# SP's order of reads and loads, the place of the block transpose, and row maxima over two banks in a perceiver layer's kernel

## The chip, the cores and the metric

The kernel runs on one core of a Trainium2 chip. The metric is the device time of one execution in microseconds. Time before: 3738.01 us, the median of 3 runs (3735.43 to 3746.63). One further execution was profiled; it took 3731.84 us, and every duration below comes from it.

The core's engines each work through a list of their own: TensorE (PE, with its weight loads PEld), VectorE (DVE), ScalarE (ACT), GpSimd (POOL) and SyncE (SP). SP computes nothing: it issues the transfers (DMAs) one after the other, and an instruction of SP that has to wait holds all that stand behind it.

## The reference

One layer on x (16 sequences of 128 rows, 512 wide), with a context of 2048 rows for each sequence, all in float32. It has three parts, each added to x after a layernorm:

```
q = ln(x) @ wq.T + bq;  k = ctx @ wk.T + bk;  v = ctx @ wv.T + bv      # 16 heads of 32
x = x + softmax(q k^T / sqrt(32)) v @ wo.T + bo                        # attention
x = x + mamba_block(ln(x))     # in_proj, causal conv, selective scan over 16 states, out_proj, then an MLP
x = x + expert_mix(ln(x))      # softmax gate, top 2, one shared and one expert matrix
```

The change lies in the attention: the scores, the softmax, and the product of the probabilities with v.

## The kernel before, in words

The work is one stream of steps (the loop at L1329). Step u handles one sequence, one quarter of its context (512 rows) and one group of four heads: 16 x 4 x 4 = 256 attention steps (NU), "live" in the code. Behind them, 54 steps later, runs the selective scan of the sequences whose attention is done; the projections in and out, the normalizations and, after step 256, the MLP and the experts are fitted into the steps by tables that map a step to functions (`loads`, `late`, `behind`, `inner` and others, filled by `put`, L1205 on). The schedule is manual: each engine gets its instructions in the order in which the program writes them, and waits are added where data or buffers need them. A tile with n buffers waits for the last reader of the tile that had its buffer before.

A step does this, in the program's order:

- SP: `load_bc` of the scan's first factor, at u % 4 of 1 or 2 the next context tiles (`load_ctx`), the table `loads` (x, weights and others), then the second `load_bc` (L1337 to L1352).
- `scores` (L302): TensorE writes four heads' scores into four PSUM banks, `banks[0..3]`, 128 rows x 512 each.
- `weighted` (L379): TensorE multiplies the probabilities of step u - 1 with v. For heads 0 to 2 they were turned on TensorE (`turn`, L354: four transposes into the head's bank, a copy to pT on ScalarE). The fourth head takes another way: VectorE transposes it in blocks of 32 (`blocks`, L334), SP writes the result to a DRAM buffer trd, and four reads bring it back in the wanted order as pd (`gathered`, L344). This head is used one step later still: step u uses the pd of u - 2.
- `gathered(u - 1)` (L1362): SP's four reads. They wait for trd's write, and for TensorE's reading of the one pd buffer in this step's `weighted`.
- `maxima` (L312): VectorE, one reduction for each bank, negated. `x_products` (L278): TensorE, two products for the k or v of the next context quarter, into the PSUM tiles pa and pc. k and v are made by a scheme of seven products and sums of quarters; each takes two steps (phase 0 and 1).
- `exps` (L319): ScalarE, one exp for each bank with the negated maximum as bias; the row sums come along.
- `inputs` on GpSimd, then the first half of the scan on VectorE (`scan(g, r, 0)`, L727: a scan, a product with bc, a memset).
- `blocks(u)` on VectorE (L1395), with SP's write to trd; `hold` copies pa on ScalarE; `decays(g, r, 1)` are two exps for the scan's second half; then `x_sums` on VectorE (L1403) adds pc and the held copy. pc can be written again after that.
- `turn` for heads 0 to 2, the second half of the scan, the `late` work (projections and the like, which use banks[3] first, then the others, pc or avp as their place), `behind` (`dt_first`, L660: a product, read by ScalarE and VectorE, in pc while k or v are made), and at the end `y_products` and `y_sums`.

The weights share one ring of six tiles of 256 KB (tag "ws", WS = 6): wq and wo (`load_w`), win for the scan's input projection (`load_win`, two a step), wout for its output (`load_wout`, six at a time). Their users are in the `late` table of the following step.

Of the kernel before, what the change touches and what calls it, by code (L numbers as in the profile page):

```python
# [15 lines left out]
P = 128  # L16
# [20 lines left out]
def perceiver_layer(ctx: ExitStack, tc: tile.TileContext, a: dict, out: bass.AP):  # L37
# [75 lines left out]
    with ExitStack() as es:  # L113
# [12 lines left out]

        banks = [psum.tile([P, 512], FP, tag=f"s{j}", name=f"bank{j}") for j in range(4)]
        avp = psum.tile([P, 4, P], FP, tag="av", name="avp")  # L130
        hst = psum.tile([P, NH // 2, GT], FP, tag="h0", name="hst")
        pa = psum.tile([P, 2, 256], FP, tag="pa", name="pa")
# [33 lines left out]
        def load_w(i, b):  # L166

            for c in range(KC):
                t = ssm.tile([P, KC, P], FP, tag="ws", name=f"wqo{i}_{b}_{c}", bufs=WS)
                if i == 0:  # L170
                    nc.sync.dma_start(t, a["wqkvo"][i][:, :, c * P : (c + 1) * P])
                else:
                    nc.sync.dma_start(t.rearrange("p a b -> p (a b)"), a["wqkvo"][i][:, c, :])
                wts_in[i, b, c] = t
# [113 lines left out]
        def x_sums(of, g, ph, pa, pc):  # L288
            sums[of](g, ph, ph, pc, held[of])
# [21 lines left out]

        def maxima(u):  # L312
            b, sb, hg = split(u)
            for j in range(4):
                nc.vector.tensor_reduce(  # L315
                    stats[b][0][j][:, sb, hg : hg + 1], banks[j], AX.X, ALU.max, negate=True
                )

        def exps(u):  # L319
            b, sb, hg = split(u)  # L320
            nm, sm = stats[b]
            pr = pool.tile([P, 4, 512], FP, tag="pr", name=f"pr{u}", bufs=1)
            for j in range(4):
                h = hg * 4 + j
                nc.scalar.activation(  # L325
                    pr[:, j, :],
                    banks[j],
                    AF.Exp,
                    bias=nm[j][:, sb, hg : hg + 1],
                    accum_out=sm[:, sb, h : h + 1],  # L330
                )
            prs[u] = pr

        def blocks(u):  # L334

            t = pool.tile([P, 4, ND, 4, 32], FP, tag="tr", name=f"tr{u}", bufs=1)
            for h in range(ND):
                nc.vector.transpose(  # L338
                    t[:, :, h].rearrange("p c i q -> p i c q"),
                    prs[u][:, NP + h, :].rearrange("p (i c k) -> p i c k", i=4, c=4),  # L340
                )
            nc.sync.dma_start(trd[u % 2], t.rearrange("p c h i q -> p (c h i q)"))

        def gathered(u):  # L344
# [70 lines left out]
        def normal(b):  # L415

            x = xts[b]
            root_third(rstd[:, b : b + 1], *xts.pop((b, "r")))
            xn = keep.tile([P, D], FP, tag="aT", name="xn", bufs=1)
            nc.vector.tensor_scalar(  # L420
                xn, x, mv[:, b, 0:1], rstd[:, b : b + 1], ALU.subtract, ALU.mult
            )
            if b:
                nc.gpsimd.tensor_tensor(x, x, bo, ALU.add)
            xts[b, "n"] = xn
            nm = [keep.tile([P, SB, 4], FP, tag=f"nm{j}", name=f"nm{b}_{j}") for j in range(4)]
            sm = keep.tile([P, SB, H], FP, tag="sm", name=f"sm{b}")
            stats[b] = nm, sm

# [31 lines left out]
        def joined(b):  # L461

            parts, sm = stats[b]
            nm = keep.tile([P, SB, H], FP, tag="nm", name=f"nm{b}")
            for j in range(4):
                nc.vector.tensor_copy(
                    nm.rearrange("p s (k j) -> p s k j", j=4)[:, :, :, j], parts[j]
                )
            stats[b] = nm, sm

# [74 lines left out]
        def load_win(g, i):  # L545

            t = ssm.tile([P, KC, P], FP, tag="ws", name=f"win{g}_{i}", bufs=WS)
            nc.sync.dma_start(t, a["win"][i // 4][:, :, (i % 4) * P : (i % 4 + 1) * P])
            wts_in[g, i] = t
# [650 lines left out]


        early = {}
        late, after, inner, middle, loads, head, behind, between = ({} for _ in range(8))

        def put(where, u, f):  # L1205
            where.setdefault(u, []).append(f)

        for b in range(B):
            s = 16 * b
            if b:  # L1210
                put(loads, s - 8, lambda b=b: load_x(b))
                put(loads, s - 5, lambda b=b: load_w(0, b))
                put(inner, s - 8, lambda b=b: moments_of(b))
                put(middle, s - 7, lambda b=b: root_of(b))
                put(inner, s - 7, lambda b=b: normal(b))
                put(late, s - 4, lambda ps, b=b: queries(b, ps))
            e = s + 16
            put(loads, e + 5, lambda b=b: load_w(3, b))
            put(inner, e - 1, lambda b=b: joined(b))
            put(inner, e, lambda b=b: joined_first(b))  # L1220
            put(middle, e + 1, lambda b=b: shares(b))
            put(inner, e + 1, lambda b=b: joined_second(b))
            put(head, e + 2, lambda b=b: joined_third(b))
            for sb in range(SB):
                put(inner, e + 2 + (sb > 0), lambda b=b, sb=sb: spread_out(b, sb))
                put(late, e + 3 + (sb > 0), lambda ps, b=b, sb=sb: scaled(b, sb, ps))
            put(late, e + 6, lambda ps, b=b: attended(b, ps))
            put(middle, e + 7, lambda b=b: root_of(b))
            put(inner, e + 7, lambda b=b: normed(b))
            put(late, e + 8, lambda ps, b=b: z_turned(b, ps))  # L1230
        for g in range(NG):
            p = 32 * (g + 1)
            for ec in range(EC):
                put(loads, p + 8 + ec, lambda g=g, ec=ec: load_win(g, ec))
                put(loads, p + 8 + ec, lambda g=g, ec=ec: load_win(g, EC + ec))
                put(late, p + 9 + ec, lambda ps, g=g, ec=ec: x_part(g, ec, ps))
                put(late, p + 9 + ec, lambda ps, g=g, ec=ec: z_part(g, ec, ps))
                put(after, p + 10 + ec, lambda g=g, ec=ec: silu_first(g, ec, xas))
                put(after, p + Z_GATES[ec], lambda g=g, ec=ec: silu_first(g, ec, zss))
            put(late, p + 18 + (g == NG - 1), lambda ps, g=g: x_proj(g, ps))  # L1240
            s = p + LAG
            for ec in range(EC):
                put(loads, s - 4 + 4 * ec, lambda ec=ec: load_dtproj(ec))
                put(behind, s - 3 + 4 * ec, lambda ps, g=g, ec=ec: dt_first(g, ec, ps))
                put(middle, s - 2 + 4 * ec, lambda g=g, ec=ec: dt_second(g, ec))
                put(between, s - 1 + 4 * ec, lambda g=g, ec=ec: dt_third(g, ec))
            for i in range(GB):
                for ec in range(WS):
                    put(loads, s + 32 + 2 * i, lambda g=g, i=i, ec=ec: load_wout(g, i, ec))
                put(loads, s + 31 + 2 * i, lambda b=g * GB + i: reload_x(b))  # L1250
                put(late, s + 33 + 2 * i, lambda ps, g=g, i=i: projected(g, i, ps))

# [76 lines left out]
        for u in range(last):  # L1329
# [4 lines left out]
            made, phase = divmod(u + 3, 4)  # L1334
            makes = 0 < made < B * SB
            of, phase = ("k", "v")[phase // 2], phase % 2
            load_bc(u + 2 - 32 - LAG, 0)  # L1337
            if u % 4 == 1 and made + 1 < B * SB:
                load_ctx(made + 1, ("c00", "c10", "c11"))
            if u % 4 == 2 and made + 1 < B * SB:  # L1340
                load_ctx(made + 1, ("c01",))
            for f in loads.get(u, ()):
                f()
            if scans and u <= NU:
                decays(g, r, 0)
            if u > NU:
# [2 lines left out]
                    fed += 1  # L1349
                if scans:  # L1350
                    decays(g, r, 0)
            load_bc(u + 1 - 32 - LAG, DS)  # L1352
            if u == NU + 1:
                load_rows()
            if live:
# [1 line left out]
            if 1 <= u <= NU:  # L1357
                weighted(u - 1, range(4))
                if u > 1:
                    weighted_last(u - 2)  # L1360
                weighted_out(u - 1)
                gathered(u - 1)  # L1362
            for f in early.get(u, ()):
                f()
            if u == NU:
# [25 lines left out]
            silu_third()  # L1391
            if scans:
                scan(g, r, 0)
            if live:
                blocks(u)  # L1395
            if live and u % 4 == 2:
                values_kept(u // 4)
            if makes:
# [2 lines left out]
                decays(g, r, 1)  # L1401
            if makes:
                x_sums(of, made, phase, pa, pc)  # L1403

# [8 lines left out]

            ahead = live and u % 16 in (3, 10) and len(after_turns) == 1
            if ahead:
                after_turns[0](banks[3])
                after_turns, places = (), ()
            if live:  # L1420
                for j in range(NP):
# [10 lines left out]
                    f(ps)  # L1432
                    give_back(ps)
            for f in behind.get(u, ()):
                ps = flat(pc) if makes else banks[2] if live else bank()
                f(ps)
                if not live:
                    give_back(ps)
# [84 lines left out]
```

## Time and profile before

| | |
|---|---|
| profiled execution | 3731.84 us |
| its span, first to last instruction | 3730.1 us |
| median of the runs | 3738.01 us |
| mean granted TensorE clock | 0.992 |
| step 0 starts / step 255 starts | 42.15 / 3041.25 us |
| one reduction of 128 x 512 (L315), 1024 of them | 681 ns |
| one exp of 128 x 512 (L325), 1024 of them | 686 ns |
| the block transpose of 128 x 512 (L338), 256 of them | 711 ns |
| first sum of a k part, 128 x 256 (L264), 256 of them | 461 ns |
| the same of v, 128 x 512 (L274), 126 of them | 663 ns |
| bc load, 512 KB, issue to landing (median) | 4.9 us |
| pd read, 64 KB, issue to landing (median) | 2.6 us |
| SP waits at the pd reads for TensorE | 555.9 us, 209 times |

A line of a view names engine, source line, operation, out<-in, and the number of instructions (x8). In the timeline the first two numbers are the start and the length in us of a run of such instructions, and in brackets stands the engine's idle time before it and what ended it. In the list of waits the numbers are the sum in us, how often, and the longest. In the windows view follow, after the stretch and its length, the busy times of PE, PEld, DVE, ACT and POOL, then the granted clock of TensorE (1.00 is full), the busy share of the DMA engines, and GB/s. "SPq" is SP's queue. Times written as "scores + 5.6" are counted from the start of a step's first scores matmul.

### The profile page before, as it was taken

The page shows a single profiled execution, that of the slowest core. Times are in us where ns is not written, and L with a number is a line of the kernel's source. Part 1 is how long each engine was busy: PE and PEld are TensorE (multiplying, and loading weights), DVE is VectorE, ACT ScalarE, POOL GpSimd, SP SyncE. Part 2 cuts the span into 40 slices and gives each one's busy share as a digit, 9 for nine tenths or more (in the row PEclk, how much of TensorE's full clock was granted, in tenths as well). Part 3 has the DMA queues.
Part 4 walks back from the last instruction along what each step waited for, and adds up shares of the span by engine and source line. Part 5 has one row for each costly group of instructions (what it writes and reads, how often), then busy time and mean ns, then how long its engine had stood idle before and what let it go on. Part 6 is the DMA issues. An engine that isn't in the chain of part 4 may idle for free.

```text
span 3730.1 us, 71240 instructions
## 1 busy us (share of the span) xinstructions
PE 3643.5 (98%) x25096; PEld 2762.6 (74%) x25096; DVE 2712.5 (73%) x4902; ACT 2423.5 (65%) x5928; POOL 2135.2 (57%) x2097
## 2 busy tenths in 40 slices
PE   9999999999999999999999999999999989999999
PEld 7878787777777877778777867787777766655655
DVE  4444546887778787878687878877887777778843
ACT  4555556776677776777686767776777675545432
POOL 2111114774767576766676667666675667667820
PEclk9999999999999999999999999999999999999999
DMA  4323334565566556565756565656565668577752
GB/s 126 94 91 97 114 97 145 188 210 160 190 209 201 182 188 204 184 195 166 223 181 198 166 226 177 193 173 218 187 199 177 205 208 320 196 272 240 249 191 81
DMA packets 527556, 682.76 MB, mean 183 GB/s; under 512 B 44848, under 2 KB 378960, under 8 KB 526944
## 3 DMA queue, kind: packets, MB, share of 16 engines
q1 hardware_dynamic: 526752, 677.57, 56.5%
q8 instruction: 200, 3.28, 0.4%
q14 instruction: 156, 1.28, 0.1%
q0 software_dynamic: 448, 0.63, 0.1%
HBM read 594.40 MB, written 83.62 MB: 182 GB/s over the span
## 4 chain that ended last, share of the span: by engine, by line
PE 91%; DMA 3%; DVE 2%; ACT 1%; SPq 1%; issue 1%; POOL 0%; DVEq 0%; ACTq 0%; POOLq 0%
PE pa L244 24%; PE pc L244 17%; PE bank L358 8%; PE avp L386 7%; PE bank L307 7%; PE bank L575 5%; PE bank L986 4%; PE bank L955 3%; PE bank L760 2%; PE bank L1087 2%; DMA pd<-trd 2%; PE bank L516 2%; PE bank L443 1%; PE avp L986 1%; PE pa L955 1%
## 5 line engine op out<-in xcount | busy, mean ns | idle before, releaser
L315 DVE TENSOR_REDUCE nm<-bank 128x1 f32<-128x512 f32 x1024 | 634.9, 681 | 263.8 <-PE bank L307 263.1
L747 POOL TENSOR_TENSOR ysum<-ysum,w 128x512 f32<-128x512 f32 x384 | 499.9, 1302 | 453.3 <-DVE hst L710 262.3
L325 ACT ACTIVATE pr<-bank,nm 128x512 f32<-128x512 f32 x1024 | 689.1, 686 | 65.9 <-DVE nm L315 61.1
L696 POOL TENSOR_TENSOR w<-dx,bc 128x512 f32<-128x512 f32 x512 | 654.7, 1300 | 8.9
L731 DVE TENSOR_TENSOR_SCAN hst<-hst,w 128x512 f32<-128x512 f32 x459 | 561.0, 1222 | 43.7 <-ACT hst L717 39.2
L717 ACT ACTIVATE hst<-dt,alog 128x254 f32<-128x254 f32 x918 | 440.1, 479 | 79.2 <-DVE hst L710 63.9
L360 ACT COPY pT<-bank 128x512 f32<-128x512 f32 x768 | 396.6, 587 | 51.3 <-PE bank L358 51.0
L358 PE MATMUL bank<-ident,pr 128*128 128x128 f32 x3072 | 378.2, 273 | 0.8 <-ACT pr L325 0.7
L358 PEld LDWEIGHTS bank<-ident,pr 128*128 128x128 f32 x3072 | 350.5, 141 | 26.3 <-ACT pr L325 3.0
L386 PEld LDWEIGHTS avp<-pT,v 128*32 128x32 f32 x6144 | 206.5, 110 | 193.7 <-issue 193.0
L734 DVE TENSOR_TENSOR w<-hst,bc 128x512 f32<-128x512 f32 x459 | 317.2, 691 | 20.9 <-DMA bc<-bcd 5.3
L236 POOL TENSOR_TENSOR t<-c,c 128x512 f32<-128x512 f32 x128 | 164.3, 1284 | 239.9 <-PE pc L244 235.1
L307 PE MATMUL bank<-kt,qT 32*128 32x512 f32 x2048 | 295.7, 640 | 0.7 <-ACT pT L360 0.7
L386 PE MATMUL avp<-pT,v 128*32 128x128 f32 x6144 | 280.8, 277 | 0.0
L338 DVE STREAM_TRANSPOSE tr<-pr 128x512 f32<-128x512 f32 x256 | 182.1, 711 | 102.2 <-ACT pr L325 101.2
L244 PE MATMUL pa<-vs,t 128*128 128x256 f32 x1008 | 252.5, 395 | 0.0
L244 PE MATMUL pa<-t,ks 128*128 128x256 f32 x1024 | 248.6, 386 | 0.0
L386 PE MATMUL avp<-pd,v 128*32 128x128 f32 x1536 | 206.4, 278 | 38.1 <-DMA pd<-trd 38.1
L244 PEld LDWEIGHTS pa<-vs,t 128*128 128x128 f32 x1008 | 190.7, 195 | 37.1 <-issue 11.9
L244 PEld LDWEIGHTS pa<-t,ks 128*128 128x128 f32 x1024 | 185.9, 190 | 36.0 <-issue 14.2
L325 ACT ACTIVATION_READ_ACCUMULATOR pr<-bank,nm 128x1 f32 x1024 | 208.5, 204 | 0.0
L623 POOL TENSOR_TENSOR xa<-xa,sg 128x256 f32<-128x256 f32 x64 | 46.7, 729 | 263.7 <-ACT sg L622 263.7
(321 smaller groups left out, 7524.3 us busy)
## 6 DMA issues: line engine op xcount, KB each, us to landing
bc<-bcd SPq DMA_DIRECT2D x512, 512.0 KB, 4.9
c<-in_ctxT_dram SPq DMA_DIRECT2D x256, 256.0 KB, 4.8
trd<-tr SPq DMA_DIRECT2D x256, 256.0 KB, 2.1
pd<-trd SPq DMA_DIRECT2D x1024, 64.0 KB, 2.6
wf<-in_w_dram SPq DMA_DIRECT2D x124, 512.0 KB, 6.7
wqo<-in_wqkvo_dram SPq DMA_DIRECT2D x128, 256.0 KB, 5.3
win<-in_win_dram SPq DMA_DIRECT2D x128, 256.0 KB, 5.0
wout<-in_wout_dram SPq DMA_DIRECT2D x128, 256.0 KB, 4.1
```

Of the source, the lines that this page charges most:

```text
L244: nc.tensor.matmul(ps[:, r, :], l[:, kc, r * P : (r + 1) * P], m[:, kc, :], start=(i in (1, 2, 5) and r == 0 and kc == 0), stop=(r == 1 an ...
L307: nc.tensor.matmul(banks[j], qts[b][rows, hg, :], kts[u // 4, hg][rows, :], start=True, stop=True)
L315: nc.vector.tensor_reduce(stats[b][0][j][:, sb, hg : hg + 1], banks[j], AX.X, ALU.max, negate=True)
L325: nc.scalar.activation(pr[:, j, :], banks[j], AF.Exp, bias=nm[j][:, sb, hg : hg + 1], accum_out=sm[:, sb, h : h + 1],)
L358: nc.tensor.transpose(ps[:, i, :], prs[u][:, j, i * P : (i + 1) * P], ident)
L360: nc.scalar.copy(pT, ps)
L386: nc.tensor.matmul(avp[j * HD : (j + 1) * HD, v % 4, :], values(v, i, j), pts[v, j][:, i, :] if j < NP else pds[v][:, :, j - NP, i, :], st ...
L696: nc.gpsimd.tensor_tensor(w, dx.unsqueeze(1).to_broadcast([P, NH // 2, GT]), bcs[g * 32 + r, 0][:, i * NH // 2 : (i + 1) * NH // 2, :], AL ...
L717: nc.scalar.activation(bt(h[:, k, :])[:, :, 1:], bt(dt)[:, :, 1:], AF.Exp, scale=aneg[:, ec, n : n + 1],)
L731: nc.vector.tensor_tensor_scan(flat, flat, w.rearrange("p n t -> p (n t)"), 0.0, ALU.mult, ALU.add)
L734: nc.vector.tensor_tensor(w, h, bcs[g * 32 + r, DS][:, i * NH // 2 : (i + 1) * NH // 2, :], ALU.mult)
L747: nc.gpsimd.tensor_tensor(s, s, w, ALU.add)
```

## The change

- **SP's order.** In steps 1 to 256 the loads of a step no longer come first. They become `step_loads`, called after `gathered(u - 1)`: the table `loads`, both `load_bc`, then `load_ctx`. The weights of the ring move to a table of their own, `weights`, which runs at the end of the engines' middle part, behind trd's write. In the steps after 256 the weights go with `step_loads` at the start of the step, and both `load_bc` stand behind them, ahead of what `feed` loads.
- **VectorE's order.** `blocks(u)` comes after `x_sums` (and after `decays` and `values_kept`), no longer ahead of them. The transpose itself is one call for all its heads; with one such head it is the same instruction as before.
- **Maxima.** The four banks become two PSUM tiles of two banks each; `banks[j]` is a slice of one. `maxima` makes two reductions of 128 x 2 x 512 in place of four of 128 x 512. The statistics tiles and their joining change with it (two copies in place of four).
- **Places.** `dt_first` uses banks[3], where a step has no late work, and otherwise its place of before. The line with `after_turns[0](free[0])` names the same bank as before (NP is 3).

```diff
-        banks = [psum.tile([P, 512], FP, tag=f"s{j}", name=f"bank{j}") for j in range(4)]
+        pairs = [psum.tile([P, 2, 512], FP, tag=f"s{m}", name=f"bank{m}") for m in range(2)]
+        banks = [pairs[j // 2][:, j % 2, :] for j in range(4)]
...
-            for j in range(4):
+            for m in range(2):
                 nc.vector.tensor_reduce(
-                    stats[b][0][j][:, sb, hg : hg + 1], banks[j], AX.X, ALU.max, negate=True
+                    stats[b][0][m][:, sb, hg, :], pairs[m], AX.X, ALU.max, negate=True
                 )
...
-                    bias=nm[j][:, sb, hg : hg + 1],
+                    bias=nm[j // 2][:, sb, hg, j % 2 : j % 2 + 1],
...
-            for h in range(ND):
-                nc.vector.transpose(
-                    t[:, :, h].rearrange("p c i q -> p i c q"),
-                    prs[u][:, NP + h, :].rearrange("p (i c k) -> p i c k", i=4, c=4),
-                )
+            nc.vector.transpose(
+                t.rearrange("p c h i q -> p (h i) c q"),
+                prs[u][:, NP:, :].rearrange("p h (i c k) -> p (h i) c k", i=4, c=4),
+            )
...
-                put(loads, s - 5, lambda b=b: load_w(0, b))
+                put(weights, s - 5, lambda b=b: load_w(0, b))
...
-            put(loads, e + 5, lambda b=b: load_w(3, b))
+            put(weights, e + 5, lambda b=b: load_w(3, b))
...
-                put(loads, p + 8 + ec, lambda g=g, ec=ec: load_win(g, ec))
-                put(loads, p + 8 + ec, lambda g=g, ec=ec: load_win(g, EC + ec))
+                put(weights, p + 8 + ec, lambda g=g, ec=ec: load_win(g, ec))
+                put(weights, p + 8 + ec, lambda g=g, ec=ec: load_win(g, EC + ec))
...
-                    put(loads, s + 32 + 2 * i, lambda g=g, i=i, ec=ec: load_wout(g, i, ec))
+                    put(weights, s + 32 + 2 * i, lambda g=g, i=i, ec=ec: load_wout(g, i, ec))
...
-            load_bc(u + 2 - 32 - LAG, 0)
-            if u % 4 == 1 and made + 1 < B * SB:
-                load_ctx(made + 1, ("c00", "c10", "c11"))
-            if u % 4 == 2 and made + 1 < B * SB:
-                load_ctx(made + 1, ("c01",))
-            for f in loads.get(u, ()):
-                f()
+
+            def step_loads():
+                for f in loads.get(u, ()):
+                    f()
+                for f in weights.get(u, ()) if u > NU else ():
+                    f()
+                load_bc(u + 2 - 32 - LAG, 0)
+                load_bc(u + 1 - 32 - LAG, DS)
+                if u % 4 == 1 and made + 1 < B * SB:
+                    load_ctx(made + 1, ("c00", "c10", "c11"))
+                if u % 4 == 2 and made + 1 < B * SB:
+                    load_ctx(made + 1, ("c01",))
+
+            if not 1 <= u <= NU:
+                step_loads()
...
-            load_bc(u + 1 - 32 - LAG, DS)
...
                 gathered(u - 1)
+                step_loads()
...
-            if live:
-                blocks(u)
...
             if makes:
                 x_sums(of, made, phase, pa, pc)
+            if live:
+                blocks(u)
+            for f in weights.get(u, ()) if u <= NU else ():
+                f()
...
-                after_turns[0](banks[3])
+                after_turns[0](free[0])
...
-                ps = flat(pc) if makes else banks[2] if live else bank()
+                n = len(late.get(u, ()))
+                if live and n < len(free):
+                    ps = free[n]
+                else:
+                    ps = flat(pc) if makes else banks[2] if live else bank()
```

More of the change, by code (lines that the diff above doesn't have):

```diff
@@ L425, in normal @@
             xts[b, "n"] = xn
-            nm = [keep.tile([P, SB, 4], FP, tag=f"nm{j}", name=f"nm{b}_{j}") for j in range(4)]
+            nm = [
+                keep.tile([P, SB, 4, 2], FP, tag=f"nm{m}", name=f"nm{b}_{m}") for m in range(2)
+            ]
             sm = keep.tile([P, SB, H], FP, tag="sm", name=f"sm{b}")
@@ L464, in joined @@
             nm = keep.tile([P, SB, H], FP, tag="nm", name=f"nm{b}")
-            for j in range(4):
+            for m in range(2):
                 nc.vector.tensor_copy(
-                    nm.rearrange("p s (k j) -> p s k j", j=4)[:, :, :, j], parts[j]
+                    nm.rearrange("p s (k m j) -> p s k m j", m=2, j=2)[:, :, :, m, :], parts[m]
                 )
@@ L1202, in perceiver_layer @@
         early = {}
-        late, after, inner, middle, loads, head, behind, between = ({} for _ in range(8))
+        late, after, inner, middle, loads, head, behind, between, weights = ({} for _ in range(9))
         def put(where, u, f):
```

## The prediction

> **What bounds it now.** First the page: engines, then the chain that ended last.
>
> ```profile
> PE 3643.5 (98%) x25096; PEld 2762.6 (74%) x25096; DVE 2712.5 (73%) x4902; ACT 2423.5 (65%) x5928; POOL 2135.2 (57%) x2097
> ...
> PE 91%; DMA 3%; DVE 2%; ACT 1%; SPq 1%; issue 1%; POOL 0%; DVEq 0%; ACTq 0%; POOLq 0%
> ```
>
> TensorE carries the end, and its idle time is only 3730.1 - 3643.5 = 86.6 us. So a gain must come out of that time, or out of matmuls that run slow. Next, the waits of TensorE:
>
> ```profile
> PE avp L386 <- DMA pd<-trd: 40.1, 16, 3.8
> PE pc L244 <- DVE kt L264: 7.4, 8, 1.2
> ```
>
> Half of the idle time is one wait: the fourth head's probabilities (pd) come late from DRAM. The timeline shows where. TensorE in step 108 (a step runs from one group of scores, L307, to the next):
>
> ```profile
> 1248.18 1.14 PE L307 MATMUL bank<-kt,qT 32*128 32x512 f32 x8
> 1249.26 0.42 PE L386 MATMUL avp<-pT,v 128*32 128x128 f32 x6
> 1252.17 0.27 PE L386 MATMUL avp<-pd,v 128*32 128x128 f32 x1 [2.49 <-DMA pd<-trd]
> ...
> 1253.74 3.01 PE L244 MATMUL pa<-vs,t 128*128 128x256 f32 x8
> ```
>
> and SP's queue before it:
>
> ```profile
> 1228.42 3.85 SPq L171 DMA_DIRECT2D wqo<-in_wqkvo_dram  x4
> 1244.40 2.27 SPq L548 DMA_DIRECT2D win<-in_win_dram  x2
> 1246.76 0.57 SPq L645 DMA_DIRECT2D bc<-bcd  x1
> 1247.38 1.85 SPq L348 DMA_DIRECT2D pd<-trd  x4
> ```
>
> From 1232.27 to 1244.40 SP waits to load win: its ring of six tiles is full until the in_proj of 1242.48 has read one. The four reads of pd stand behind it, although their data lay ready. In step 119 six wout loads (L553) do the same. The gaps at pd lie in steps 12 and 23 of every 32 (u mod 32), twelve in all, 36.7 us.
>
> A stall costs more than itself: the 8 products after this one took 3.01 us, elsewhere 1.89 to 1.99. The windows view of 10 us around stalls has the granted clock after the engines:
>
> ```profile
> 1250.00:1260.00 10.00, 7.83 (x58) 6.72 (x59) 5.90 (x10) 6.03 (x18) 2.58 (x3) 0.83 0.31 102
> 862.00:872.00 10.00, 6.99 (x43) 5.70 (x43) 4.37 (x7) 4.98 (x14) 1.88 (x3) 0.66 0.33 110
> 1006.00:1016.00 10.00, 7.67 (x59) 6.08 (x60) 6.35 (x10) 5.82 (x17) 2.13 (x3) 1.00 0.69 239
> ```
>
> 0.83 over 10 us is 1.7 us lost, 0.66 is 3.4, 1.00 nothing. Nine of the twelve windows read 0.83, two 0.66, one 1.00: 9 x 1.7 + 2 x 3.4 = 22.1 us.
>
> The Trainium skill ("TensorE: Matmul & The Clock Gate", section "What's actually happening") says the clock falls to half after an idle window of about 3.4 us. Here nine of the ten stalls shorter than that were followed by a slow window, so the rows overrule it. By the rule only the stalls of 3.45 and 3.77 us would pay, 3.4 us in all, and the first term below would be about 20 us smaller.
>
> **The change, part by part.**
>
> *1. SP's order: gathers first, weights last.* In step u (1 to 256) SP now has the four reads of pd (u-1), then loads, bc and ctx, then trd's write, then weights. The waits for the ring (win, wout, wqo) no longer stand ahead of the reads within a step. They could only delay the next step's reads, and those wait for its weighted anyway (scores + 2.2 us). Worst cases by step time: in 11 the second win waits for in_proj until +10.5, SP is free at 11.2, the next reads are due at 12.66 + 2.2; in 22 wout waits for the out projection until +10.4, next reads at 13.9 + 2.2. So the stalls go whole. Their size by step length: step 108 took 22.03; step 92 with the same queries but no in_proj took 14.07, and an in_proj pair adds 3.45 (step 109's 12.22 less step 117's 8.77), so 17.52. The six steps 12 sum to 136.56, 31.4 over. Step 25 (projection) takes 15.64, dt_first adds 0.55, so step 23 should take 16.19; the six sum to 126.44, 29.3 over. Together **-60.7 us** (36.7 idle and 22.1 slow clock give 58.8: the two ways agree). Two single gaps at pd, 1.22 us at 494.73 and 1.75 at 3059.56, go for the most part, as bc no longer lies ahead of pd in the DMA queue (pd landed there 4.7 us after issue, in quiet steps 2 to 2.6): **-2.7**.
>
> What the moved DMAs pay: bc and ctx are issued at about scores + 4.2, behind the reads (4 x 0.46 us), no longer ahead of the step. bc lands about 5 us after issue: the second bc at about +10. Its first reader, the product after the next step's first scan, starts 4.81 into a step of 8.77 or more: 13.6, so 3.6 us to spare. The first bc feeds POOL one step, and the scan two steps, later. ctx has three steps, x is read by bn_stats at +9.3 and should land by +8. Weights go out from +7.6 and land by +12 (two tiles) to +16 (six); they are due behind the turns of the next step, +15.7 at the earliest and +17.9 where there are six. All hidden by TensorE's own step: 0. SP's issues sum to about 7 us of 8.77.
>
> In the tail (257 on) weights and loads go ahead of both bc, and bc ahead of the feed's wf. win rarely waits there and wf is two units early: 0, from -8 to +8 by the size of its single stalls (2 to 4.6 us).
>
> *2. x_sums ahead of the block transpose.* VectorE reached x_sums 0.7 us later than pc was done, as the transpose (0.71) came first. In step 98 (2 mod 32) this makes TensorE wait 1.07 us and more. Now the sums start at the latest of pc (scores + 5.80), the memset (5.5) and the held copy. Steps 2 gain 0.54 (the maxima begin late there, so the held copy sets it), steps 30 gain 0.29, steps 0 0.19, steps 26 0.13: 6 x (0.54 + 0.29 + 0.19 + 0.13) = **-6.9**. The transpose, and with it trd, comes 0.6 to 0.8 us later, with a step's slack ahead of the reads. VectorE idles about 0.3 us for pc, so the second scan starts about 0.3 later (0.4 where a sigmoid's exp delays the held copy).
>
> *3. Maxima of two banks.* No reduce of 1024 is in the trace. One of 512 takes 681 ns, one of 64 (L475) 253: the slope gives 681 + 512 x 0.955 = 1170; double is 1362, and a scan of 512 takes 1222. I take 1215 (between slope and double, nearer the slope); ends 681 and 2444 (twice the scan's row). VectorE gains some 0.13 us a step; the first exp starts 0.53 later. Its cover: in steps 1 mod 4, the shortest, the exps wait for the copy of avp until 2.50 anyway and the first pair ends at 2.38; in 0 mod 4 they wait until 2.75. In 2 and 3 mod 4 the turns start at 5.64 with exps done at 5.2, and the pT copies end at about 8.6 against the next scores at 9.32 or later. Cost 0 to a reduce of 1.6 us; beyond it the pT copies (8.44 of 8.77) delay the scores.
>
> *4. dt_first into bank 3* where a step has no late work: u = 27, 31, 7 mod 32, 19 steps with products. Before, it used pc, which is next written 3.9 us into the next step; bank 3 is due with the next scores. VectorE's reader (L670) ended at 9.29, 9.30 and 9.42 of 9.32; 0.3 to 0.4 later and with 0.05 for the semaphore the scores of head 3 wait 0.32 in 27 and 31, 0.46 in 7: 13 x 0.32 + 6 x 0.46 = **+6.9** (0 to +12). The other use of free[0] is bank 3 as before.
>
> *5. Two copies instead of four in joined* (297 ns each): VectorE is idle near there, 0.
>
> Sum: -60.7 - 2.7 - 6.9 + 6.9 = -63.4. The profiled execution took 3731.84 (span 3730.1), so 3668.4; it lies 6.2 under the runs' median 3738.01. On that median: **3674.6 us**.
>
> **Rivals.**
>
> *A. The loads behind the gathers come late.* bc follows up to 1.5 MB of weights from the step before; at the 334 GB/s of a full stretch (1248.2 to 1252.2) these take 4.5 us, and the second bc's 3.6 us to spare is gone. For it: both DMA share and SP's order are tight in steps 8 to 15. Against: weights are issued at +7.6, so most have landed before the next bc. If 0.3 us reaches TensorE in the 14 of 32 steps with weights, some 98 steps, 29 us come back: 3704.
>
> *B. The pair makes waits coarse; slower.* The two banks are now one tile. If its waits hold for the tile, late work in bank 3 waits for the copy of bank 2 (ends 8.4, late work starts 6.95): 1.4 us in 21 of 32 steps, 130 steps, +182 - 63: 3857. It decides above 0.5 us a step. Against: the four heads' pr is one tile too, and in step 0 the first turn starts at 44.86, before the second exp is done (45.4).
>
> *C. It doesn't do what it says:* the reads stay late, because stores or the ring still hold SP over the next step's start. For it: SP waited 12 us for one slot. Against: the deadlines above. The stalls stay, terms 2 and 4 cancel: 3738.
>
> **Chances.** Forecast 0.72, A 0.12, B 0.07, C 0.09. My forecast's own bounds: dt_first's 0 and 8 us of the tail below (3660), 8 of the tail and 5 of dt_first above (3688), with the runs' spread (3735.43 to 3746.63) some 5 us wider. The range takes in A: 3655 to 3706. A measurement of this kernel tells about 0.3% from no change: faster 0.72 + 0.12 + a little of C = 0.85, same 0.07, slower 0.08.
>
> **What would show it.** Right: no wait of avp for pd over 0.5 us in steps 12 and 23, whose lengths fall to about 17.5 and 16.2; no slow clock between 860 and 2960; steps 2 near 11.3; TensorE's busy time lower by some 22 us; SP's reads ahead of bc; steps 27, 31, 7 at 9.6 to 9.8. Wrong: reduces over 1.6 us, a new wait of TensorE for pT, of the scan for bc, of late work for pT, or steps of 8.77 that have grown.

## The result and the profile after

The changed kernel takes **4254.83 us** (median of 4 runs, 4251.21 to 4260.39); the kernel before took 3742.32 in the same comparison (3735.43 to 3747.41). The ratio is 1.1372, with an interval of 1.1346 to 1.1398: 13.7% slower, where the forecast was 1.7% faster. The profiled execution of the changed kernel has a span of 4251.6 us, 521.5 more than before.

The page of the changed kernel: the engines, the chain that ended last, and two groups (busy, mean ns | idle time just ahead, and who ended it).

```profile
PE 3765.8 (89%) x25096; PEld 2777.5 (65%) x25096; DVE 2663.6 (63%) x4358; ACT 2440.8 (57%) x5928; POOL 2127.3 (50%) x2097
...
PE 57%; ACT 30%; DVE 8%; issue 3%; DMA 1%; SPq 0%; DVEq 0%; ACTq 0%
...
L316 DVE TENSOR_REDUCE nm<-bank 128x2 f32<-128x1024 f32 x512 | 602.2, 1217 | 366.2 <-PE bank L308 366.2
L358 PE MATMUL bank<-ident,pr 128*128 128x128 f32 x3072 | 436.7, 278 | 297.3 <-ACT pT L360 294.4
```

TensorE was 98% busy and carried 91% of the chain; now it is 89% busy and ScalarE has 30% of the chain. TensorE's idle time went from 86.6 to 4251.6 - 3765.8 = 485.8 us, which is 399.2 of the 521.5. Its busy time grew by the other 122.3, with the same 25096 matmuls. The new reduction is no surprise (1217 ns). The last line is: ahead of the transposes of the heads' probabilities (L358, "the turns") TensorE now stands idle for 297 us. The same line of the kernel before has 0.8:

```profile
L358 PE MATMUL bank<-ident,pr 128*128 128x128 f32 x3072 | 378.2, 273 | 0.8 <-ACT pr L325 0.7
```

The waits of TensorE in the changed kernel (us in total, times, longest):

```profile
PE bank L358 <- ACT pT L360: 294.4, 256, 2.2
PE bank L577 <- ACT pT L360: 30.6, 42, 0.8
PE bank L665 <- ACT pT L360: 15.2, 21, 0.7
...
PE bank L518 <- ACT pT L360: 11.0, 15, 0.8
PE bank L570 <- ACT pT L360: 10.9, 15, 0.7
PE bank L762 <- ACT pT L360: 8.7, 12, 0.7
```

Neither of the two waits that the prediction started from is there: pd and kt are gone from the list. The new ones in the attention steps are nearly all for one instruction, the copy of a turned head from PSUM to pT (L360), and the first occurs 256 times, once in each step. (The steps after attention have new waits of their own, for VectorE and ScalarE, of 13.6 us and less.) One step of the changed kernel, step 92, shows them. First TensorE, then ScalarE:

```profile
1211.21 1.89 PE L245 MATMUL pc<-vs,t 128*128 128x256 f32 x8
1212.94 0.60 PE L358 MATMUL bank<-ident,pr 128*128 128x128 f32 x4
1214.75 1.09 PE L358 MATMUL bank<-ident,pr 128*128 128x128 f32 x8 [1.21 <-ACT pT L360]
1216.57 2.14 PE L445 MATMUL bank<-xnT,wqo 128*128 128x128 f32 x9 [0.73 <-ACT pT L360]
```

```profile
1213.17 1.01 ACT L719 ACTIVATE hst<-dt,alog 128x254 f32<-128x254 f32 x2
1214.12 0.58 ACT L360 COPY pT<-bank 128x512 f32<-128x512 f32 x1
1215.44 1.07 ACT L360 COPY pT<-bank 128x512 f32<-128x512 f32 x2 [0.75 <-PE bank L358]
```

The kernel before in its step 92, TensorE and then ScalarE's copies:

```profile
1075.88 1.47 PE L358 MATMUL bank<-ident,pr 128*128 128x128 f32 x12
1077.19 3.74 PE L443 MATMUL bank<-xnT,wqo 128*128 128x128 f32 x32
...
1077.07 1.54 ACT L360 COPY pT<-bank 128x512 f32<-128x512 f32 x3
```

There the 12 matmuls of three heads run as one group, and the late work (L443) starts behind them while the copies are still under way. In the changed kernel head 0's four (into bank 0) end at 1213.54, and head 1's, into bank 1, start at 1214.75, 0.05 after head 0's copy has ended (1214.12 + 0.58 = 1214.70). Nothing of head 1's data is in that copy: what the two share is the tile, banks 0 and 1. The late work in bank 3 starts at 1216.57, 0.06 after the end of the copies (1215.44 + 1.07 = 1216.51), the second of which reads bank 2, its tile's other half. And the copy of head 0 itself is late because ScalarE has two exponentials of the scan (1.01 us) queued ahead of it: these cost nothing as long as nobody waited for the copy.

The windows view of the tail, from 12 us after the start of step 255 to the end, of the changed kernel and then of the kernel before (time, busy time of PE, PEld, DVE, ACT, POOL, granted clock, DMA share, GB/s):

```profile
3489.50:4251.60 762.10, 677.76 (x2294) 421.58 (x2294) 453.47 (x925) 302.87 (x628) 387.48 (x356) 0.95 0.58 198
```

```profile
3053.25:3730.10 676.85, 648.84 (x2292) 410.59 (x2284) 458.84 (x927) 303.81 (x627) 390.77 (x356) 0.99 0.65 223
```

The tail uses the same banks for its own products, and it lost 85.3 us: 56.3 of TensorE's idle time (84.3 against 28.0), the rest in matmuls at a lower granted clock. So by stages: attention 437.5 us longer, the tail 85.3, the start 1.3 shorter.

### The profile page after: what moved, and what is told of

It reads as the page before. It is cut to its first block, busy times and chain, and to the rows that moved or that the text cites. A ratio compares the mean times of both kernels' runs of the same rounds, so it can differ in the third digit from the quotient of the medians.

```text
span 4251.6 us, 70653 instructions
## 1 busy us (share of the span) xinstructions
PE 3765.8 (89%) x25096; PEld 2777.5 (65%) x25096; DVE 2663.6 (63%) x4358; ACT 2440.8 (57%) x5928; POOL 2127.3 (50%) x2097
## 4 chain that ended last, share of the span: by engine, by line
PE 57%; ACT 30%; DVE 8%; issue 3%; DMA 1%; SPq 0%; DVEq 0%; ACTq 0%
ACT pr L326 13%; PE pa L245 12%; PE pc L245 7%; ACT pT L360 7%; PE bank L308 6%; PE bank L358 6%; ACT hst L719 5%; PE bank L577 5%; DVE nm L316 3%; PE avp L386 3%; PE bank L988 3%; PE bank L1089 2%; PE bank L957 2%; PE bank L518 2%; PE bank L762 1%
## 5 line engine op out<-in xcount | busy, mean ns | idle before, releaser
L316 DVE TENSOR_REDUCE nm<-bank 128x2 f32<-128x1024 f32 x512 | 602.2, 1217 | 366.2 <-PE bank L308 366.2
L358 PE MATMUL bank<-ident,pr 128*128 128x128 f32 x3072 | 436.7, 278 | 297.3 <-ACT pT L360 294.4
L358 PEld LDWEIGHTS bank<-ident,pr 128*128 128x128 f32 x3072 | 347.3, 141 | 384.3 <-ACT pT L360 355.0
L360 ACT COPY pT<-bank 128x512 f32<-128x512 f32 x768 | 423.2, 584 | 222.6 <-PE bank L358 222.5
L577 PE MATMUL bank<-zT,win 128*128 128x256 f32 x808 | 207.5, 411 | 36.8 <-ACT pT L360 30.6
L577 PEld LDWEIGHTS bank<-zT,win 128*128 128x128 f32 x808 | 161.3, 205 | 72.3 <-ACT pT L360 40.6
```

What stands on the lines that cost most here:

```text
L316: nc.vector.tensor_reduce(stats[b][0][m][:, sb, hg, :], pairs[m], AX.X, ALU.max, negate=True)
L358: nc.tensor.transpose(ps[:, i, :], prs[u][:, j, i * P : (i + 1) * P], ident)
L360: nc.scalar.copy(pT, ps)
L577: nc.tensor.matmul(ps, w[:, kc, :], zTs[g][:, kc, :], start=(kc == 0), stop=(kc == KC - 1))
```

## Experiments

Ten kernels ran. The theories, by the numbers that the expectations use: **1**, the shared two-bank tile makes its users wait for each other; **2**, the reduction of 1024 is what is dear; **3**, the new order of SP and VectorE makes ScalarE late. For what SP's order alone gave, **4** says that the loads it moved (bc and ctx) push other transfers back; its rival 5 is in the expectations that name it. In the diffs "before" and "after" name the kernel that is edited.

### Four one-bank tiles (e1_four_tiles)

The whole change without its third part: four tiles and four reductions of 512 again.

```
-        pairs = [psum.tile([P, 2, 512], FP, tag=f"s{m}", name=f"bank{m}") for m in range(2)]
-        banks = [pairs[j // 2][:, j % 2, :] for j in range(4)]
+        banks = [psum.tile([P, 512], FP, tag=f"s{j}", name=f"bank{j}") for j in range(4)]
...
-            for m in range(2):
+            for j in range(4):
```

> The changed kernel with only its maxima part undone: four PSUM tiles of one bank, four reductions. Theory 1 (the wait comes from two banks being one tile: a write to one bank waits for the reader of the other): the waits of the turns and of the work in bank 3 for pT (294 + 96 us) go, also those of the steps after 256, and the time is the forecast's, 3660 to 3690 us. Theory 2 (the reduction of 1024 delays the exps, these the pT copies): the same here. Theory 3 (SP's order or the sums ahead of the transpose make ScalarE late): still over 4100 us.

Measured: 3721.49 us, 0.9954 of before (0.9939 to 0.9969). TensorE has no wait for pT ahead of the turns any more. The 533 us between this and the changed kernel belong to the third part. But what is left of the change gives 16.8 us, not 63.4.

### The tiles alone (e2_pair_tiles)

The kernel before, with only these two lines changed. The four reductions stay, each of 512 elements of one bank.

```
-        banks = [psum.tile([P, 512], FP, tag=f"s{j}", name=f"bank{j}") for j in range(4)]
+        pairs = [psum.tile([P, 2, 512], FP, tag=f"s{m}", name=f"bank{m}") for m in range(2)]
+        banks = [pairs[j // 2][:, j % 2, :] for j in range(4)]
```

> The kernel before with one edit: the four banks are slices of two tiles of two banks; the four reductions of 512 stay. Theory 1: the turn of head 1 waits for head 0's pT copy in all 256 steps (about 1.15 us), late work in bank 3 for head 2's copy (0.7 us); 4200 to 4330 us, that is some 500 to 580 over the kernel before. Theory 2 and theory 3: 3740 us, no change.

Measured: 4307.73 us, 1.1526 (1.1504 to 1.1548). No instruction of the computation has changed, only which PSUM tile a bank is a part of. The waits of TensorE in this kernel:

```profile
PE bank L359 <- ACT pT L361: 301.0, 256, 2.3
PE avp L387 <- DMA pd<-trd: 38.9, 13, 3.6
PE bank L576 <- ACT pT L361: 30.6, 42, 0.8
```

The same 256 waits, and the old wait for pd beside them. Theory 3 falls, since the order is the old one here.

The trace also shows that the program itself makes the engines wait, with signals (semaphores, by which one engine tells another that it is done). In the kernel before, the scores of each of the four heads signal that they are written, in all 256 steps. Here only two of the four do, those of the second head of each pair: one signal for a tile. And where the trace has all of a step's records (254 steps), head 1's turn starts 0.05 us after the end of head 0's copy. So the wait comes from how the program is put together around the tile, with no instruction that got slower.

### The maxima part alone (e3_pair_maxima)

The kernel before with the whole third part: e2's tiles and

```
-            for j in range(4):
+            for m in range(2):
                 nc.vector.tensor_reduce(
-                    stats[b][0][j][:, sb, hg : hg + 1], banks[j], AX.X, ALU.max, negate=True
+                    stats[b][0][m][:, sb, hg, :], pairs[m], AX.X, ALU.max, negate=True
```

> The kernel before with the whole maxima part: two tiles of two banks and two reductions of 1024. Theory 1: within 1% of the kernel that has the two tiles and four reductions; the reduction of 1024 takes 1.22 us as in the changed kernel. Theory 2: slow only here, and not with four reductions. Theory 3: 3740 us.

Measured: 4300.12 us, 1.1504 (1.1476 to 1.1532), with 287.6 us of the same waits at the turns. The intervals of e2 and e3 overlap, so two reductions of 1024 (1218 ns each here) in place of four of 512 make no difference that these runs tell. Theory 2 falls.

### Turns in another order (e8_turns_021)

The changed kernel, with head 1 turned last. Then the tile of banks 0 and 1 rests during the turn of head 2, and bank 2 is copied out before the late work asks for bank 3.

```
-                for j in range(NP):
+                for j in (0, 2, 1):
```

> The changed kernel, its turns in the order of heads 0, 2, 1: neighbours in time now lie in different two-bank tiles. Theory 1: the third turn still waits for head 0's copy, but the second no longer waits, and the work in bank 3 waits for a copy that is done 0.5 us earlier: 4030 to 4180 us. If the turns waited for the pT copies for another reason than the shared tile: 4250 us, no change.

Measured: 4042.5 us, 1.0811 (1.0784 to 1.0838). This kernel's largest wait of TensorE:

```profile
PE bank L358 <- ACT pT L360: 178.1, 232, 2.0
```

The wait shrinks by 116 us, to 0.77 us a time, and the late work no longer waits for pT at all. Which of two turns waits is settled by which one shares a tile with the other: theory 1 again, by an edit that touches no tile.

### SP's order alone (e4_sp_order)

The kernel before with the first part of the change: reads, then loads, bc and ctx, then trd's write, then weights.

```
-            load_bc(u + 2 - 32 - LAG, 0)
...
-            for f in loads.get(u, ()):
-                f()
+            def step_loads():
...
                 gathered(u - 1)
+                step_loads()
...
+            for f in weights.get(u, ()) if u <= NU else ():
+                f()
```

> The kernel before with SP's new order alone (reads first, loads behind them, weights last). The prediction's term: -63.4 us (60.7 for steps 12 and 23, 2.7 for two single gaps), so 3675 to 3685 us, steps 12 near 17.5 us and steps 23 near 16.2, no wait for pd over 0.5 us in the attention steps. Rival A (the loads behind the reads come late): 3700 or more, with waits of the scan or of GpSimd for bc that reach TensorE.

Measured: 3724.55 us, 0.9965 (0.9947 to 0.9983): 13.7 us gained, not 63.4. By differences of step lengths between the two traces (u mod 32): steps 12 gained 31.4 us, just as forecast; steps 23 gained 14.7 of 29.3; steps 25 lost 24.3, steps 22 lost 1.8, steps 253 and 254 lost 6.5. The waits of TensorE name the loser:

```profile
PE bank L759 <- DMA wout<-in_wout_dram: 25.3, 12, 3.6
```

L759 is the out projection. It reads eight wout tiles, and the last two are issued within it, when the ring has room. TensorE and SP's queue of this kernel in step 121:

```profile
1418.84 5.32 PE L759 MATMUL bank<-wout,zs 128*128 128x512 f32 x12
1426.62 3.67 PE L759 MATMUL bank<-wout,zs 128*128 128x512 f32 x4 [2.46 <-DMA wout<-in_wout_dram]
```

```profile
1414.11 2.75 SPq L347 DMA_DIRECT2D pd<-trd  x4
1416.96 0.86 SPq L644 DMA_DIRECT2D bc<-bcd  x2
1417.87 1.70 SPq L158 DMA_DIRECT2D c<-in_ctxT_dram  x3
1419.67 0.57 SPq L341 DMA_DIRECT2D trd<-tr  x1
1420.34 0.99 SPq L552 DMA_DIRECT2D wout<-in_wout_dram  x2
```

Both bc (512 KB each), three ctx tiles and trd (256 KB each) now go out within the 3.4 us ahead of these two loads, which land 6.2 us after issue. Steps 23 hold an out projection too: six of the 12 waits are theirs (10.4 us), the other six lie in steps 25 (14.9 us). In the kernel before, bc went out at the step's start, and the same loads, issued 0.2 us later in the step, landed after 2.9 us. So the transfers that were moved from ahead of the reads did not vanish; they moved to the front of wout. In steps 252 to 254 the scan waits for bc itself (4.1 us once), which delays ScalarE's copies of pT and so the next scores: rival A's mechanism, at one place. On GpSimd bc is late more often, 19 times and 30.3 us in all, where the kernel before has no such wait.

### Weights last, the rest as it was (e9_weights_last)

The kernel before, with the weights' table taken out of the start of the step and put at its end. bc, ctx and the x loads stay where they were, ahead of the reads.

```
-                put(loads, p + 8 + ec, lambda g=g, ec=ec: load_win(g, ec))
+                put(weights, p + 8 + ec, lambda g=g, ec=ec: load_win(g, ec))
...
+            for f in weights.get(u, ()) if u <= NU else ():
+                f()
```

> The kernel before with half of SP's new order: the weights go behind trd's write at the end of the step, while bc, ctx, x and the rest stay at the start, ahead of the reads. Theory 4 (bc and ctx, moved behind the reads, lie ahead of the projection's last two wout loads in the DMA queue, and these then come late): the stalls at pd go as in the kernel with SP's whole order, the waits for wout do not come, 3675 to 3690 us. Theory 5 (the waits for wout come from the weights' own later place): waits for wout as there, 3715 to 3730 us.

Measured: **3675.23 us** (3674.28 to 3675.9), 0.9828 (0.9814 to 0.9843). It beats both kernels: 63.8 us under before. Steps 12 gain 31.4 us, steps 23 gain 30.0, steps 25 lose 2.1. The engines, two of the waits of TensorE, and SP's queue in step 108 (from 1236.17), the step whose stall the prediction showed:

```profile
PE 3624.5 (99%) x25096; PEld 2747.9 (75%) x25096; DVE 2708.4 (74%) x4902; ACT 2421.7 (66%) x5928; POOL 2134.1 (58%) x2097
```

```profile
PE avp L760 <- DMA wout<-in_wout_dram: 2.7, 1, 2.7
...
PE bank L760 <- DMA wout<-in_wout_dram: 1.2, 2, 0.9
```

```profile
1238.39 1.74 SPq L348 DMA_DIRECT2D pd<-trd  x4
1242.59 0.34 SPq L342 DMA_DIRECT2D trd<-tr  x1
1244.21 1.44 SPq L548 DMA_DIRECT2D win<-in_win_dram  x2
1245.74 0.57 SPq L645 DMA_DIRECT2D bc<-bcd  x1
1246.36 6.08 SPq L158 DMA_DIRECT2D c<-in_ctxT_dram  x3
```

TensorE idles 48.6 us in all. The reads go out 2.2 us after the step's start, and only then come the two win loads. bc and ctx follow at the start of the next step's list, ahead of its reads, and no wait of TensorE for pd is left in this kernel. Of the 12 waits of the out projection in e4 two are left, 1.2 us in all (the one of 2.7 us comes after the attention steps). Theory 4 holds and its rival falls: what helps here is to take the loads that are held up by the ring from ahead of the reads; what hurt was to move bc and ctx too.

### The same with VectorE's new order (e10_weights_sums)

e9, and x_sums ahead of the block transpose.

```
-            if live:
-                blocks(u)
...
                 x_sums(of, made, phase, pa, pc)
+            if live:
+                blocks(u)
```

> The one above with x_sums ahead of the block transpose too, four tiles and four reductions, dt_first in its old place. Theory 4 and the prediction's term for the sums: 3668 to 3685 us, 5 to 9 below the one above, steps 2 mod 32 near 11.3 us. If the transpose, 0.6 us later, makes trd or the scan late: equal or above.

Measured: 3679.39 us, 0.984 (0.9818 to 0.9862), not below e9. Steps 0, 26 and 30 gain 5.0 us together, steps 23 and 25 lose 12.2: the transpose and so trd's write come later (8.3 us into step 121, where e9 has 7.3), the weights wait behind that write on SP, and the out projection waits for wout again (10.5 us in 8 waits). A gain on VectorE was paid back on SP's queue.

### VectorE's order alone (e5_sums_first)

The kernel before, with the edit of e10.

> The kernel before with x_sums ahead of the block transpose, nothing else. The prediction's term: -6.9 us, 3731 to 3733, by steps 2, 30, 0 and 26 mod 32. The rival, that trd's write, later by some 0.7 us and with it all that stands behind it in SP's queue, costs TensorE as much in the steps with the projection: 3738 to 3745 us.

Measured: 3729.83 us (11 runs), 0.9976 (0.9967 to 0.9985), 8.2 us gained of a forecast 6.9. But it isn't the sum that was forecast. Steps 30 gain 1.8 us, steps 26 gain 1.4 and steps 0 gain 1.0, while steps 2, which should have given 3.2, gain only 0.4: TensorE waits there as long as before (1.0 to 1.07 us). The other half of the gain lies in small differences scattered over the steps, and I can't tell it from scatter in the profile.

### The projection's place alone (e6_bank3_only)

The kernel before, with dt_first in bank 3 where no late work takes it.

```
-                ps = flat(pc) if makes else banks[2] if live else bank()
+                n = len(late.get(u, ()))
+                if live and n < len(free):
+                    ps = free[n]
+                else:
+                    ps = flat(pc) if makes else banks[2] if live else bank()
```

> The kernel before with dt_first in bank 3 where a step has no late work, nothing else. The sums are not yet ahead of the transpose, so VectorE's reader ends 0.2 to 0.3 us earlier than in the changed kernel: the scores after steps 27, 31 and 7 wait about 0.05 to 0.15 us each, +1 to +3 us, 3739 to 3741. If the scores' wait is for the whole reader chain at its place in the changed kernel (0.2 to 0.4 us): +6.5 us.

Measured: 3740.32 us (11 runs), 1.0005 (0.9996 to 1.0014): +2.3 us, which the interval doesn't tell from nothing.

### The change without tiles and without bank 3 (e7_no_bank3)

e1 with dt_first in its old place, so SP's order and VectorE's order together.

```
-                n = len(late.get(u, ()))
-                if live and n < len(free):
-                    ps = free[n]
-                else:
-                    ps = flat(pc) if makes else banks[2] if live else bank()
+                ps = flat(pc) if makes else banks[2] if live else bank()
```

> The changed kernel with four tiles and four reductions, and dt_first in its old place: SP's order and the sums' order alone. The prediction's term for dt_first in bank 3 is +6.9 us: so 6 to 7 us under the kernel with four tiles alone (3721.5), 3714 to 3716; the steps after 27, 31 and 7 lose the 0.2 to 0.4 us that they had gained there.

Measured: 3711.95 us, 0.9928 (0.9914 to 0.9943), 9.5 us below e1. Between their traces steps 0, 8 and 28 are each 0.4 to 0.5 us shorter, six of a kind, 7.8 us together. So bank 3 costs 8 to 9.5 us behind VectorE's new order and about 2, within the noise, without it. VectorE's reader of the bank (`dt_first`'s second reader) ends 9.59 us into steps 27 and 31 in e1, and 9.30 in e6.

## Why the prediction was wrong

**The step that failed most is rival B's price and its chance (0.07).** The mechanism was named: the two banks are one tile, and its waits may hold for the tile. Two things went wrong.

- The argument against it was that pr, one tile for four heads, lets a turn start before the next head's exponential is done. That holds for pr, which lies in SBUF, and it didn't carry over to this PSUM tile: e2 shows 256 waits from the tile alone, and one signal for a tile of two banks. Why this program's waits go by parts for the one and by the whole for the other, the runs don't show; that stays open. The row should have set a bound, not a chance.
- The price counted the late work in bank 3 only: 1.4 us in 130 steps, 182 us. That wait came to 0.69 us in 135 (93.2 us; five kinds are shown above, three smaller ones come to 16.8), half the forecast, since the first wait has by then pushed the late work itself back (in step 92 it asks for bank 3 8.5 us into the step, where the forecast had 6.95). Left out was the other pair. Banks 0 and 1 are two successive turns, so head 1's turn waits for head 0's copy in each of 256 steps: 294.4 us. Left out too was the tail, which uses the same banks: 85.3. That cost comes with the tile as well: from the start of step 255 to the end the kernel before takes 688.8 us, e1 692.2, e2 776.3.

How the 521.5 us add up by the profile: TensorE's idle time +399.2, of which 294.4 + 93.2 are waits for pT and 56.3 lie in the tail, against some 40 saved at pd and small differences elsewhere; busy time +122.3, of which 58.5 is the turns' own (436.7 against 378.2 us, since one group of 12 became 4 and 8) and most of the rest slower matmuls at a lower clock.

**Term 1, SP's order (-60.7, -2.7), failed at "What the moved DMAs pay: 0".** Its stalls went as worked out: steps 12 by 31.4 of 31.4, steps 23 by 30.0 of 29.3 where the wout loads were not late (e9). But the step looked at when the moved bc and ctx land, and at when the weights land, each by itself. It took weights issued at +7.6 and due in the next step; it missed the two wout loads that are issued within the projection and due 3.8 us later (1420.34 to 1424.16 in step 121 of e4), behind 2 MB just put on the same queue. With bc and ctx moved, the part gains 13.7 (e4); with them left, 63.8 (e9).

**Term 2 (-6.9)** came to -8.2 alone, right in size and half wrong in place: steps 2 gave 0.4 of 3.2, so the match in size is in part luck. And it isn't free in company: "with a step's slack ahead of the reads" is right of the reads, but the weights now stand behind trd's write (e10).

**Term 3 (cost 0)** was right for the reduction, 1217 ns against the 1215 taken, and for its cover (e3 is no slower than e2). That the reduction came within 2 ns is in part luck: 1215 was chosen between bounds of 1170 and 1362, and the lower one leans on a reduction of another kind (L475, a minimum read out of SBUF). The cost of the term lay in the tile that it needs, which the step didn't price.

**Term 4 (+6.9)** was about right in company (+8 to +9.5) and too much alone (+2.3, within the noise). **Term 5** (the joined copies) was not measured by itself; e3 has it and is no slower than e2.

**Rival C** (stalls stay) was wrong: no wait for pd is left in steps 12 and 23 of any kernel that has the weights at the end.

## What to carry to other kernels

When several buffers are merged into one tile, list every pair of users that were independent and now share it, in each stage that uses the buffers, and price the wait of each pair in turn; the operation that the merge serves may be the smallest part of the bill. When DMAs are reordered on a queue, price not only when the moved ones land but what each of the others now has ahead of it, above all a late load that is issued just before its use. Here it paid to move the loads that blocked the queue and to leave the others where they were.

## What the runs showed of the hardware that I had not expected

In these traces the granted clock falls by idle time summed over a window, not by one long gap. In step 92 of the changed kernel no gap is longer than 1.21 us. The windows view of the 3.41 us up to the end of its two gaps, and of the next 3.41 us (columns as above; PE busy first, granted clock after POOL):

```profile
1213.35:1216.76 3.41, 1.47 (x11) 1.05 (x10) 3.33 (x6) 2.63 (x6) 0.82 (x2) 1.00 0.85 296
1216.76:1220.17 3.41, 3.41 (x17) 3.41 (x17) 0.19 (x1) 0.07 (x1) 3.33 (x3) 0.50 0.01 3
```

TensorE was idle for 57% of the first, and the second ran at 0.50 with TensorE busy throughout. The length of 3.41 us is that of the slow stretches themselves: 25 of the changed kernel's 36 last so long, and most others a multiple of it. Cutting the whole trace into such windows and counting: of 51 that were idle by half or more, 43 were followed by one at half clock; of the other 1192, 4 were. In the kernel before it was 16 of 18 and 2 of 1071. That it is the sum and not the gap shows in the windows of the changed kernel whose longest gap inside them was between 1.2 and 1.7 us: with half or more idle in all, 13 of 14 were followed by half clock, with less, none of 91. The changed kernel spent 161 us at half clock, the kernel before 61.

The Trainium skill ("TensorE: Matmul & The Clock Gate", section "HAM oscillation — how this bites in real kernels") gives the rule as no idle gaps over about 3.4 us. These windows differ: gaps of 1.21 and 0.73 us were enough, and here the measurement decides. The sum also fits what the prediction had met without a reason, that stalls of 2.5 us at pd were followed by a slow window.
